# Turning x and h of a graph network by DMA crossbar transfers instead of TensorE

## The chip, the cores and the metric

The kernel runs on one core of a Trainium2 chip. The metric is the device time in microseconds (us); before the change it is 2685.53 us, the median of three runs (2683.47 to 2687.09). The engines are PE (TensorE, matmul), DVE (VectorE), ACT (ScalarE), POOL (GpSimd) and SP (SyncE, which here only issues DMA transfers).

## The reference

The input x is 128 graphs of 128 nodes with 256 features, in fp32; adj is a 128x128 adjacency matrix per graph. Four layers follow each other, each with a residual sum and a layer norm over the features. Layer 0 is a gated graph network of three steps, layers 1 to 3 are attention layers on the graph.

```python
# layer 0
A = (adj != 0)
h = x
for i in range(3):
    m = h @ weight[i]
    aggr = einsum('bst,bsd->btd', A, m)
    gi = aggr @ w_ih.T + b_ih
    gh = h @ w_hh.T + b_hh
    r = sigmoid(i_r + h_r); z = sigmoid(i_z + h_z)
    n = tanh(i_n + r * h_n)
    h = (1 - z) * n + z * h
x = layernorm(x + h)
# layers 1 to 3, in outline
Wh = x @ W.T
e = leaky_relu(Wh @ a1 + (Wh @ a2).T), masked where adj == 0
x = layernorm(x + softmax(e) @ Wh)
```

## The kernel before

The 128 graphs are worked on in 32 groups of 4 (G = 4), so that a tile of 128 partitions has 4 x 128 = 512 columns (GN). The 256 features are two halves of 128 (KC = 2, index c).

A group goes through gru() (layer 0) and then gat() (layers 1 to 3). gru() needs the node state h in two layouts. In rows (nodes on partitions, features along the row) h is the stationary operand of the aggregation at line 526, A transposed times h. Turned (features on partitions, the nodes of 4 graphs along the row) it is the moving operand of the gate products at line 473, and the elementwise work on the gates is done in this layout too. So x, which is loaded in rows, is turned at the start (transposed(), line 372; the PE transposes at line 380), and the new h, which arises turned, is brought back to rows after steps 0 and 1 (line 607). After step 2 the same line 607 turns h for the layer norm. A PE transpose is a matmul against the identity of one 128x128 block; four of them fill a PSUM bank, and one copy of 128x512 (line 287 on ACT or 289 on DVE, by copy()) takes the bank to an SBUF tile.

The gate products use a scheme with 7 block products in place of 8 (strassen(), line 456; sums(), line 433, makes the sums of the moving operand on GpSimd or DVE, line 443). A gate bank is emptied by lines 534, 538 and 541 on ACT and line 478 on DVE. The new h is made by lines 568 to 591; line 586 may run on GpSimd or DVE. In gat(), lines 711 and 722 are the two matmuls of the attention, 648 and 681 its PE transposes.

The order of the work is planned before the build. Every operation is given to the class Plan with the engines that may do it and an assumed duration for each, the tiles it reads and writes, and a priority (by group). Plan.order() starts operations one after another on the engine that is free, with assumed hand-over times (LATENCY: 250 for PE, 220 ACT, 200 DVE, 250 POOL, 4000 SP, in ns, and a margin of 300 ahead of PE), and the instructions are emitted in this order. Each engine then works through its own list strictly in order; an instruction whose inputs are not there holds everything behind it on its engine. Buffers come from pools of fixed size: "gate" and "bank" are the 8 PSUM banks, "k2" are SBUF tiles of 128x512 fp32, "k4" of 128x1024. `own` sets how many buffers of a pool the older of the groups in work keeps for itself.

In the steady part of the run gru() of one group and gat() of another share PE. The last four groups (LAST = 4) are ordered step by step instead of group by group.

Of the kernel before, what the change touches and what calls it, by code (L numbers as in the profile page):

```python
# [14 lines left out]
P = 128  # L15
D = 256
KC = D // P
G = 4
GN = G * P
H = GN // 2  # L20
STEPS = 3
# [177 lines left out]
def adj_resnorm_kernel(  # L199
# [14 lines left out]
    nc = tc.nc  # L214
    B = x.shape[0]
    NG = B // G
    LAST = 4
# [3 lines left out]
    psum = ctx.enter_context(tc.tile_pool(name="psum", bufs=1, space=bass.MemoryType.PSUM))  # L221


    pools = {"gru": 5, "xs": 2, "adj": 2, "am": 5, "k2": 26, "k4": 18, "fx": 2, "jx": 2, "f": 4, "mv": 4, "st": 6, "v": 24,
             "gate": 5, "bank": 3}
    own = ({"k2": 12, "k4": 5, "gate": 2, "v": 5, "fx": 0, "jx": 0, "st": 0}, {"k2": 4, "k4": 3, "v": 5, "fx": 0, "jx": 0, "st": 0})
    floats = {"gru": 0, "k4": 1024, "xs": 1024, "fx": 256, "jx": 256, "f": 8, "mv": 8, "st": 6, "v": 4}
    tags = {t: (n, floats.get(t, 512)) for t, n in pools.items()}
    BOTH = ("DVE", "POOL")
    plan = Plan({t: n for t, (n, _) in tags.items()}, own)  # L230
    slots = {t: [(psum if t in ("gate", "bank") else work).tile([P, w], I32 if t == "adj" else F32, name=f"{t}{i}")
# [2 lines left out]
    def T(b):  # L234
        if b.at is None:
            width = 1
            for s in b.shape:
                width *= s
            at = slots[b.tag][b.slot][:, 0:width]
            if len(b.shape) == 2:  # L240
                at = at.rearrange("p (a b) -> p a b", b=b.shape[-1])
            elif len(b.shape) == 3:
                at = at.rearrange("p (a b c) -> p a b c", b=b.shape[-2], c=b.shape[-1])
            b.at = at
        return b.at

    def bank():
        return Buf("bank", GN)
# [36 lines left out]
    def copy(e, dst, src):  # L285
        if e == "ACT":
            nc.scalar.copy(dst, src)  # L287
        else:
            nc.vector.tensor_copy(dst, src)  # L289

    LAND = 1500
    EVICT = {"ACT": 490, "DVE": 600}
    EVICT2 = {"ACT": 370, "DVE": 350}

    def load(dst, src, prio, start=0):
# [50 lines left out]
    def score_weights(l, prio):  # L346

        gatw, b_ = Buf("k2", KC, D), bank()
        load(gatw, gat_w[:, l], prio, start=30000)
        plan.op({"SP": 450}, lambda e: nc.sync.dma_start(T(gwT)[:, l], gat_wT[:, l]), writes=[(gwT, l)], prio=prio,  # L350
                lag=LAND, start=30000)

        for k in range(KC):
            st, mv = Buf("st", 6), Buf("mv", G, 2)
            plan.op({"DVE": 330}, lambda e, k=k, st=st: nc.vector.bn_stats(T(st), T(gwT)[:, l, k, :]),
                    reads=[(gwT, l)], writes=[st], prio=prio)
            plan.op({"DVE": 110}, lambda e, st=st, mv=mv: nc.vector.bn_aggr(T(mv)[:, 0, :], T(st)),
                    reads=[st], writes=[mv], prio=prio)
            plan.op({"DVE": 330}, lambda e, k=k, mv=mv: nc.vector.tensor_scalar(
                T(gwT)[:, l, k, :], T(gwT)[:, l, k, :], T(mv)[:, 0, 0:1], None, op0=ALU.subtract),  # L360
                reads=[mv, (gwT, l)], writes=[(gwT, l)], prio=prio)

        def fn(e):
            for h in range(2):
                for k in range(KC):
                    nc.tensor.matmul(T(b_)[:, h * D:(h + 1) * D], ga[:, l, k, h:h + 1].to_broadcast([P, P]),
                                     T(gatw)[:, k, :], start=(k == 0), stop=(k == KC - 1))
        plan.op({"PE": 4 * 432}, fn, reads=[gatw], writes=[b_], prio=prio)
        plan.op(EVICT, lambda e: copy(e, T(wa)[:, l, :, :].rearrange("p h d -> p (h d)"), T(b_)),
                reads=[b_], writes=[(wa, l)], prio=prio)  # L370

    def transposed(src, src_of, prio):

        res = []
        for c in range(KC):
            b_, dst = bank(), Buf("k2", GN)

            def fn(e, b_=b_, c=c):
                for b in range(G):
                    nc.tensor.transpose(T(b_)[:, b * P:(b + 1) * P], src_of(b, c), ident)  # L380
            plan.op({"PE": 440}, fn, reads=[src], writes=[b_], prio=prio)
            plan.op(EVICT, lambda e, b_=b_, dst=dst: copy(e, T(dst), T(b_)), reads=[b_], writes=[dst], prio=prio)
            res.append(dst)
        return res
# [48 lines left out]
    def sums(ms, prio):  # L433
# [5 lines left out]
        for j, (a, b, reads) in enumerate((  # L439
# [3 lines left out]
                nc.vector if e == "DVE" else nc.gpsimd).tensor_tensor(T(t)[:, j, :], a(), b(), ALU.subtract),  # L443
                reads=reads, writes=[(t, j)], prio=prio, port=BOTH)
        return t
# [53 lines left out]
    def gru(g, stage):  # L499

        xs, adj_i, am = Buf("xs", G, D), Buf("adj", G, P), Buf("am", G, P)
        prio = stage(g, 0)
# [4 lines left out]
                writes=[adj_i], prio=prio)  # L507
        if g == 0:
            input_weights(0, prio)
            hidden_weights(prio)  # L510
        plan.op({"DVE": 417}, lambda e: nc.vector.tensor_scalar(T(am), T(adj_i), 0, None, op0=ALU.not_equal),
                reads=[adj_i], writes=[am, turn], prio=prio, port=BOTH)
        hT = transposed(xs, lambda b, c: T(xs)[:, b, c * P:(c + 1) * P], prio)
        h = None
        for i in range(STEPS):
            prio = stage(g, i)
# [13 lines left out]
            last = i == STEPS - 1  # L530
# [15 lines left out]
            hT2 = []  # L546
            for c in range(KC):

                o, v, d = rz[c], nn[c], Buf("k2", GN)
# [4 lines left out]
                for gt in range(2):  # L554
                    if c == 0:
                        plan.op({"ACT": 630}, lambda e, gt=gt, o=o, tanh=tanh: tanh(gt, 0, GN, lambda: T(o)[:, gt, :]),
                                reads=[(o, 0), (o, 1)], writes=[(o, 2 + gt)], prio=prio)
                    else:
                        plan.op({"ACT": 365}, lambda e, gt=gt, tanh=tanh, rz=rz: tanh(
                            gt, 0, H, lambda: T(rz[2])[:, gt * H:(gt + 1) * H]),  # L560
                            reads=[rz[2]], writes=[(o, 4 + gt)], prio=prio)
                        plan.op({"ACT": 400}, lambda e, gt=gt, o=o, tanh=tanh: tanh(gt, H, GN, lambda: T(o)[:, gt, H:GN]),
                                reads=[(o, 1), (o, 4 + gt)], writes=[(o, 2 + gt)], prio=prio)
                if c == 1:
                    plan.op({"ACT": 370}, lambda e, v=v, nn=nn: nc.scalar.activation(
                        T(v)[:, 0, 0:H], T(nn[2])[:, 0:H], AF.Identity, bias=bhn[:, 1:2]),
                        reads=[nn[2]], writes=[(v, 0)], prio=prio)
                plan.op({"DVE": 620}, lambda e, o=o, v=v: nc.vector.scalar_tensor_tensor(  # L568
                    T(v)[:, 0, :], T(o)[:, 0, :], 1.0, T(v)[:, 0, :], op0=ALU.add, op1=ALU.mult),
                    reads=[(o, 2), (v, 0), (v, 1)], writes=[(v, 2)], prio=prio, port=BOTH)  # L570
                if c == 0:
                    plan.op({"DVE": 620}, lambda e, v=v: nc.vector.tensor_add(T(v)[:, 0, :], T(v)[:, 1, :], T(v)[:, 0, :]),
                            reads=[(v, 2)], writes=[(v, 3)], prio=prio, port=BOTH)
                else:
                    plan.op({"DVE": 350}, lambda e, v=v, nn=nn: nc.vector.tensor_add(
                        T(v)[:, 0, 0:H], T(nn[2])[:, H:GN], T(v)[:, 0, 0:H]),
                        reads=[(v, 2), nn[2]], writes=[(v, 3)], prio=prio)
                    plan.op({"DVE": 350}, lambda e, v=v: nc.vector.tensor_add(  # L578
                        T(v)[:, 0, H:GN], T(v)[:, 1, H:GN], T(v)[:, 0, H:GN]),
                        reads=[(v, 2)], writes=[(v, 4)], prio=prio, port=BOTH)  # L580
                plan.op({"ACT": 630}, lambda e, v=v, c=c: nc.scalar.activation(  # L581
                    T(v)[:, 0, :], T(v)[:, 0, :], AF.Tanh, bias=bin_[:, c:c + 1]),
                    reads=[(v, 3), (v, 4)], writes=[(v, 5)], prio=prio)

                plan.op({"POOL": 1250, "DVE": 610}, lambda e, d=d, v=v, h_=hT[c]: (
                    nc.vector if e == "DVE" else nc.gpsimd).tensor_tensor(T(d), T(h_), T(v)[:, 0, :], ALU.subtract),  # L586
                    reads=[hT[c], (v, 5)], writes=[d], prio=prio, port=BOTH)
                plan.op({"DVE": 620}, lambda e, d=d, o=o: nc.vector.scalar_tensor_tensor(  # L588
                    T(d), T(o)[:, 1, :], 1.0, T(d), op0=ALU.add, op1=ALU.mult),
                    reads=[(o, 3), d], writes=[d], prio=prio, port=BOTH)  # L590
                plan.op({"DVE": 620}, lambda e, d=d, v=v: nc.vector.scalar_tensor_tensor(
                    T(d), T(d), 0.5, T(v)[:, 0, :], op0=ALU.mult, op1=ALU.add),
                    reads=[d, (v, 5)], writes=[d], prio=prio, port=BOTH)
# [6 lines left out]
            else:  # L600
                h2 = [Buf("k2", G, P) for c in range(KC)]
            for c in range(KC):
                b_ = bank()

                def fn(e, b_=b_, c=c, hT2=hT2):
                    for b in range(G):
                        nc.tensor.transpose(T(b_)[:, b * P:(b + 1) * P], T(hT2[c])[:, b * P:(b + 1) * P], ident)  # L607
                plan.op({"PE": 440}, fn, reads=[hT2[c]], writes=[b_], prio=prio)
                if last:
                    plan.op({"DVE": 620}, lambda e, b_=b_, c=c, y=y: nc.vector.tensor_add(  # L610
                        T(y)[:, :, c * P:(c + 1) * P], T(b_).rearrange("p (b d) -> p b d", b=G),
                        T(y)[:, :, c * P:(c + 1) * P]), reads=[b_, turn, (y, 0)],
                        writes=[(y, b) for b in range(G)], prio=prio)
                else:
                    plan.op(EVICT, lambda e, b_=b_, c=c, h2=h2: copy(
                        e, T(h2[c]), T(b_).rearrange("p (b d) -> p b d", b=G)), reads=[b_], writes=[h2[c]], prio=prio)
            if not last:
                h, hT = h2, hT2
# [4 lines left out]
    def gat(g, xc, no, stage):  # L623
# [3 lines left out]
        for l in range(3):  # L627
# [64 lines left out]
            else:  # L692
                plan.op(EVICT, lambda e, b_=b_, pT=pT: copy(e, T(pT).rearrange("p b j -> p (b j)"), T(b_)),
                        reads=[b_], writes=[pT], prio=prio)
# [45 lines left out]
    def stage(g, n):  # L740

        tail = NG - LAST
        return g if g < tail else tail + n, 2 * g + (n >= STEPS)

    for g in range(NG):
        gat(g, *gru(g, stage), stage)
# [47 lines left out]
```

## Time and profile before

| what | value | how to read it |
|---|---|---|
| time | 2685.53 us | median of 3 runs |
| span of the profiled run | 2682.8 us | from first to last instruction |
| granted TensorE clock | 0.996 | share of full speed, so nothing is throttled |
| bank copies of 128x512 on ACT, line 287 | 396 of 587 ns | the copies after PE transposes are among them |
| the same on DVE, line 289 | 218 of 688 ns | |
| loads of x in rows | 32 of 512 KB, 3.8 us | from the issue to the landing |
| loads of adj | 32 of 256 KB, 2.8 us | the same |

Busy time of an engine is an average over the whole span; whether it matters is seen in the chain of work that ended last and in the idle time of PE. A matmul's row gives the time from its start to its end, and several are in flight at once: 128x256 products take 380 ns each by their row and follow each other every 216 ns. One matmul instruction in fp32 appears as two passes in the trace, a transpose as one.

### The profile page before, as it was taken

To read this page: it belongs to the slowest core of one execution; us is meant where nothing else is said; L and a number is where in the kernel's file an instruction comes from. 1 tells how busy PE (TensorE), PEld (TensorE's weight loads), DVE (VectorE), ACT (ScalarE), POOL (GpSimd) and SP (SyncE) were. 2 spreads that over 40 slices of the span, in tenths; PEclk is the share of its full clock that TensorE was granted. 3 is DMA by queue.
4 is the path that set the end of the run, shared out by engine and by line. 5 is a ranking of instruction groups with operands and counts; after the bars stand their busy time and mean duration, and the time that the engine had idled before them with its cause. 6 is when DMAs were issued, how large, how long until landed. Compare 5 with 4: busy or idle time off the path is not lost.

```text
span 2682.8 us, 41895 instructions
## 1 busy us (share of the span) xinstructions
PE 2650.4 (99%) x14536; PEld 2367.5 (88%) x14536; DVE 2069.0 (77%) x6111; ACT 1611.6 (60%) x4453; POOL 549.7 (20%) x618
## 2 busy tenths in 40 slices
PE   8999999999999999999999999999999999999988
PEld 7888888898898888898889888988988898988877
DVE  5677677887777877778877778777878777786787
ACT  4555666565656666566556566656666665655467
POOL 1122122221122221122211122211222211231111
PEclk9999999999999999999999999999999999999999
DMA  3100000000000000000000001000000000000000
GB/s 110 32 17 20 28 13 28 21 25 28 14 27 21 24 28 21 21 28 21 24 28 21 21 20 28 24 22 19 29 21 25 28 21 17 19 6 24 17 1 32
DMA packets 70102, 65.35 MB, mean 24 GB/s; under 512 B 2689, under 2 KB 68225, under 8 KB 69889
## 3 DMA queue, kind: packets, MB, share of 16 engines
q1 hardware_dynamic: 69456, 62.66, 7.7%
q8 instruction: 114, 1.87, 0.3%
q14 instruction: 100, 0.81, 0.1%
q10 hardware_dynamic: 432, 0.01, 0.0%
HBM read 45.89 MB, written 16.78 MB: 23 GB/s over the span
## 4 chain that ended last, share of the span: by engine, by line
PE 93%; DVE 4%; ACT 1%; issue 1%; DMA 0%; POOL 0%; POOLq 0%; SPq 0%; ACTq 0%; DVEq 0%
PE gate L473 63%; PE bank L722 11%; PE bank L526 6%; PE bank L711 6%; PE bank L607 3%; PE bank L681 1%; PE bank L648 1%; DVE fx L635 1%; PE bank L380 1%; PE bank L338 1%; DVE k L728 1%; DVE k L289 0%; DVE k L568 0%; DVE k L478 0%; DVE k L653 0%
## 5 line engine op out<-in xcount | busy, mean ns | idle before, releaser
L473 PE MATMUL gate<-k,whs 128*128 128x256 f32 x4032 | 1201.1, 380 | 2.4 <-DVE k L478 1.9
L473 PE MATMUL gate<-k,wcs 128*128 128x256 f32 x4032 | 1199.2, 379 | 0.0
L473 PEld LDWEIGHTS gate<-k,wcs 128*128 128x128 f32 x4032 | 766.1, 190 | 104.0
L473 PEld LDWEIGHTS gate<-k,whs 128*128 128x128 f32 x4032 | 730.4, 190 | 84.5 <-DVE k L478 3.1
L478 DVE TENSOR_TENSOR k<-gate,k 128x512 f32<-128x512 f32 x576 | 389.3, 684 | 207.9 <-PE gate L473 184.0
L287 ACT COPY k<-bank 128x512 f32<-128x512 f32 (+1 forms) x401 | 229.5, 584 | 206.8 <-PE bank L607 91.3
L722 PE MATMUL bank<-gwT,k 128*128 128x256 f32 x1536 | 348.8, 380 | 1.0 <-DVE k L289 0.8
L722 PEld LDWEIGHTS bank<-gwT,k 128*128 128x128 f32 x1536 | 290.4, 190 | 42.2 <-DVE k L289 1.8
L552 ACT ACTIVATE k<-k,brz 128x512 f32<-128x512 f32 (+1 forms) x384 | 225.6, 622 | 166.3 <-DVE k L478 164.7
L389 POOL TENSOR_TENSOR v<-v,neghalf 128x4 f32<-128x4 f32 x128 | 134.4, 1050 | 857.7 <-DVE v L428 840.3
L635 DVE SCALAR_TENSOR_TENSOR fx<-k,wa 128x256 f32<-128x256 f32 x768 | 285.9, 426 | 24.3 <-ACT k L408 24.2
L417 ACT ACTIVATE jx<-k 128x256 f32<-128x256 f32 x384 | 156.5, 408 | 231.0 <-DVE k L728 230.7
L534 ACT COPY k<-gate 128x512 f32<-128x512 f32 x288 | 167.6, 582 | 192.8 <-PE gate L473 188.4
L443 POOL TENSOR_TENSOR k<-k,k 128x256 f32<-128x256 f32 x229 | 175.9, 789 | 450.0 <-DVE k L289 223.2
L728 DVE SCALAR_TENSOR_TENSOR k<-bank,v,k 128x256 f32<-128x256 f32 x384 | 167.2, 476 | 106.8 <-PE bank L722 106.6
L289 DVE COPY k<-bank 128x512 f32<-128x512 f32 x219 | 150.1, 686 | 114.0 <-PE bank L711 88.6
L586 POOL TENSOR_TENSOR k<-k,k 128x512 f32<-128x512 f32 x90 | 133.3, 1492 | 303.4 <-ACT k L581 284.2
L711 PEld LDWEIGHTS bank<-k,k 128*128 128x128 f32 x1536 | 187.6, 194 | 7.7 <-DVE k L728 1.9
L711 PE MATMUL bank<-k,k 128*128 128x128 f32 x1536 | 191.2, 278 | 2.2 <-DVE k L728 1.1
L588 DVE SCALAR_TENSOR_TENSOR k<-k,k 128x512 f32<-128x512 f32 x192 | 170.1, 886 | 2.2 <-POOL k L586 1.1
L674 ACT ACTIVATE k<-k,v 128x128 f32<-128x128 f32 x384 | 148.9, 389 | 30.8 <-DVE v L670 30.2
L581 ACT ACTIVATE k<-k,bi 128x512 f32<-128x512 f32 x192 | 138.3, 721 | 47.1 <-DVE k L578 36.9
(86 smaller groups left out, 3012.9 us busy)
## 6 DMA issues: line engine op xcount, KB each, us to landing
xs<-in_x_dram SPq DMA_DIRECT2D x32, 512.0 KB, 3.8
k<-in_x_dram SPq DMA_DIRECT2D x32, 512.0 KB, 3.8
out_dram<-k SPq DMA_DIRECT2D x32, 512.0 KB, 2.9
adj<-in_adj_dram SPq DMA_DIRECT2D x32, 256.0 KB, 2.8
k<-in_gnn_wT_dram SPq DMA_DIRECT2D x3, 256.0 KB, 4.8
k<-in_w_ihT_dram SPq DMA_DIRECT2D x2, 384.0 KB, 5.8
k<-in_w_hhT_dram SPq DMA_DIRECT2D x2, 384.0 KB, 6.0
k<-in_gat_w_dram SPq DMA_DIRECT2D x3, 256.0 KB, 4.6
```

The source lines that it names most:

```text
L287: nc.scalar.copy(dst, src)
L443: nc.vector if e == "DVE" else nc.gpsimd).tensor_tensor(T(t)[:, j, :], a(), b(), ALU.subtract),
L473: nc.tensor.matmul(T(dst)[:, j * H:(j + 1) * H], T(w)[:, m, gt, :], moving(m, ms)[1](), start=first and n == 0, stop=n == len(todo) - 1, s ...
L478: plan.op({"DVE": 630}, lambda e: nc.vector.tensor_add(T(o)[:, :, j * H:(j + 1) * H], T(b_).rearrange("p (g n) -> p g n", g=2), T(part).re ...
L526: nc.tensor.matmul(T(b_)[:, b * P:(b + 1) * P], src, T(am)[:, b, :], start=True, stop=True)
L534: plan.op({"ACT": 500}, lambda e: nc.scalar.copy(T(dst), T(src)), reads=[src], writes=[(dst, 0), (dst, 1)], prio=prio)
L552: nc.scalar.activation(T(o)[:, gt, n0:n1], src(), AF.Tanh, bias=brz[:, gt * KC + c:gt * KC + c + 1], scale=0.5)
L588: plan.op({"DVE": 620}, lambda e, d=d, o=o: nc.vector.scalar_tensor_tensor(T(d), T(o)[:, 1, :], 1.0, T(d), op0=ALU.add, op1=ALU.mult), rea ...
L635: plan.op({"DVE": 345}, lambda e, b=b, h=h, l=l, f=f, fx=fx, xc=xc: nc.vector.scalar_tensor_tensor(T(fx), T(xc)[:, b, :], 1.0, T(wa)[:, l, ...
L711: nc.tensor.matmul(T(b_)[:, b * P:(b + 1) * P], T(xc)[:, b, c * P:(c + 1) * P], T(pT)[:, b, :], start=True, stop=True)
L722: nc.tensor.matmul(T(b_)[:, (b - b0) * D:(b - b0 + 1) * D], T(aT[k])[:, b * P:(b + 1) * P], T(gwT)[:, l, k, :], start=(k == 0), stop=(k == ...
L728: nc.vector.scalar_tensor_tensor(T(y)[:, b, :], T(b_)[:, (b - b0) * D:(b - b0 + 1) * D], T(rden)[:, b:b + 1], T(xc)[:, b, :], op0=ALU.mult ...
```

## The change

The turn of x (for groups 2 to 31) and the return of h to rows (after steps 0 and 1 of groups 0 to 27) are taken off PE. The crossbar of the DMA engines can transpose[...]. So turned() does it in three operations: a copy takes the fp32 words apart into a tile of all low 16-bit halves followed by all high halves; one transfer issued by SP transposes the 8 blocks of 128x128 halves into a second tile (rows); a copy puts low and high halves together again into the first tile. The copies run on ACT or DVE. Nothing is rounded: the halves are moved as integers. x of groups 0 and 1, h of the last four groups and the turn after step 2 stay on PE.

With this the pools are divided anew: 4 gate and 4 other PSUM banks in place of 5 and 3, one k2 tile more and one adjacency tile fewer, and other reserves for the older group. The planner gives the transfer 1200 ns on SP and then SP's hand-over time of 4000 ns, and the copies 1000 ns on ACT and 620 on DVE. The whole order comes out anew from it. The purpose is to relieve PE of these transposes.

```diff
-    pools = {"gru": 5, "xs": 2, "adj": 2, "am": 5, "k2": 26, "k4": 18, "fx": 2, "jx": 2, "f": 4, "mv": 4, "st": 6, "v": 24,
-             "gate": 5, "bank": 3}
-    own = ({"k2": 12, "k4": 5, "gate": 2, "v": 5, "fx": 0, "jx": 0, "st": 0}, {"k2": 4, "k4": 3, "v": 5, "fx": 0, "jx": 0, "st": 0})
+    pools = {"gru": 5, "xs": 2, "adj": 2, "am": 4, "k2": 27, "k4": 18, "fx": 2, "jx": 2, "f": 4, "mv": 4, "st": 6, "v": 24,
+             "gate": 4, "bank": 4}
+    own = ({"k2": 6, "k4": 5, "gate": 1, "bank": 1, "v": 5, "fx": 0, "jx": 0, "st": 0}, {"k2": 3, "k4": 1, "bank": 1, "v": 5, "fx": 0, "jx": 0, "st": 0})
...
+    U16 = mybir.dt.uint16
...
+    APART = {"ACT": 1000, "DVE": 620}
+    TURN = 0
...
+    def turned(src, key, dst, shape, prio):
+        rows = Buf("k2", GN)
+        flat = lambda: T(dst) if shape else T(dst).rearrange("p b q -> p (b q)")
+        halves_of = lambda at: at.bitcast(U16).rearrange("p (h b q) -> p h b q", h=2, b=G)
+        pairs_of = lambda at: at.bitcast(U16).rearrange("p b (q h) -> p h b q", h=2)
+        plan.op(APART, lambda e: copy(e, halves_of(flat()), pairs_of(src())), reads=[key], writes=[dst], prio=prio, port=BOTH)
+        plan.op({"SP": 1200}, lambda e: nc.sync.dma_start_transpose(
+            T(rows).bitcast(U16).rearrange("p (a q) -> p a q", q=P), flat().bitcast(U16)),
+            reads=[dst], writes=[rows], prio=prio, lag=TURN)
+        plan.op(APART, lambda e: copy(e, pairs_of(T(dst).rearrange(shape, b=G) if shape else T(dst)), halves_of(T(rows))),
+                reads=[rows], writes=[dst], prio=prio, port=BOTH)
...
-        hT = transposed(xs, lambda b, c: T(xs)[:, b, c * P:(c + 1) * P], prio)
+        if g < 2:
+            hT = transposed(xs, lambda b, c: T(xs)[:, b, c * P:(c + 1) * P], prio)
+        else:
+            hT = [Buf("k2", GN) for c in range(KC)]
+            for c in range(KC):
+                turned(lambda c=c: T(xs)[:, :, c * P:(c + 1) * P], xs, hT[c], "p (b q) -> p b q", prio)
...
             for c in range(KC):
+                if not last and g < NG - LAST:
+                    turned(lambda c=c, hT2=hT2: T(hT2[c]).rearrange("p (b q) -> p b q", b=G), hT2[c], h2[c], None, prio)
+                    continue
                 b_ = bank()
...
-        return g if g < tail else tail + n, 2 * g + (n >= STEPS)
+        return (g + (0 if n >= STEPS else 0) if g < tail else tail + n), 2 * g + (n >= STEPS)
```

## The prediction

> **What bounds the kernel now.** I read the engine shares and the slices first, then the windows of one steady group, then the chain, then the groups of the lines that the change touches, then the timeline around one transpose.
>
> ```profile
> PE 2650.4 (99%) x14536; PEld 2367.5 (88%) x14536; DVE 2069.0 (77%) x6111; ACT 1611.6 (60%) x4453; POOL 549.7 (20%) x618
> ...
> PE   8999999999999999999999999999999999999988
> ```
>
> PE is busy for 99% of the span; only the first slice and the last two fall short. A busy PE row alone proves little, since pipelined matmuls overlap, so the next view is one steady group in numbers (columns: span of the stretch, then busy time and instruction count of PE, PEld, DVE, ACT, POOL, then granted clock, DMA share, GB/s):
>
> ```profile
> 0.00:60.00 60.00, 51.95 (x230) 41.51 (x231) 34.55 (x74) 26.92 (x54) 11.99 (x19) 0.97 0.38 123
> 1081.60:1163.20 81.60, 81.60 (x453) 73.36 (x452) 64.17 (x192) 49.79 (x140) 16.86 (x19) 1.00 0.08 24
> 2550.00:2683.00 133.00, 114.33 (x626) 97.47 (x624) 108.01 (x500) 93.27 (x331) 21.16 (x25) 0.94 0.05 17
> ```
>
> The steady group (the chain's runs of gate products repeat every 81.6 us) leaves PE no idle time, DVE 17 us, ACT 32 us; the DMA engines are 92% free. PE idles only in the first 60 us (8) and the last 133 us (19).
>
> ```profile
> PE 93%; DVE 4%; ACT 1%; issue 1%; DMA 0%; POOL 0%; POOLq 0%; SPq 0%; ACTq 0%; DVEq 0%
> ...
> L607 PE MATMUL bank<-ident,k 128*128 128x128 f32 x768 | 115.9, 274 | 2.3 <-ACT k L287 1.5 <-DVE k L591 0.7 <-DVE k L728 0.2
> L380 PE MATMUL bank<-ident,xs 128*128 128x128 f32 x256 | 39.1, 280 | 8.3 <-DMA xs<-in_x_dram 8.0 <-ACT k L287 0.2
> ```
>
> 93% of the chain is PE: removing PE work shortens the kernel one for one until another wait appears. Lines 607 and 380 are the transposes. Their 274 ns is the time of one, not what it takes from the queue; that is read from start to start:
>
> ```profile
> 1199.92 0.60 PE L607 MATMUL bank<-ident,k 128*128 128x128 f32 x4
> ...
> 1200.36 0.60 PE L473 MATMUL gate<-k,whs 128*128 128x256 f32 x2
> ...
> 1200.56 0.59 ACT L287 COPY k<-bank 128x512 f32<-128x512 f32 x1 [1.54 <-PE bank L607]
> ```
>
> Four transposes start at 1199.92 and the next product at 1200.36: 0.44 us for one half (c) of a group. The copy out of the bank takes 0.59 us.
>
> **What the Trainium skill says.** (1) "TensorE: Matmul & The Clock Gate", Part 4: a PE transpose of 128x128 takes about 275 ns in a kernel. The trace agrees as to duration (274), but pipelined it costs 110 ns of the queue, and that is what a saving is counted in. (2) "VectorE: DVE Perf Modes", Mode 2×_2P: a one-source copy between SBUF tiles runs at two elements a cycle. The trace agrees for one such shape: line 511 takes 420 ns for 512 elements where the two-source line 591 takes 689. No 16-bit copy with a step of two is in the trace. (3) Same page, The three transpose paths: 1309 ns for a crossbar transpose of one 128x128 of 2-byte elements. (4) "DMA: Bandwidth & Descriptors", Latency and other measured facts: 261 GB/s for crossbar transposes. No run of before shows either; where the two are far apart my range is wide.
>
> **The change, part by part.**
>
> *PE work removed.* x of groups 2 to 31 (30 groups x 2 halves = 60) and h after steps 0 and 1 of groups 0 to 27 (28 x 2 x 2 = 112): 172 sets. The built instruction lists agree: 172 crossbar transposes, 688 fewer matmuls. 172 x 0.44 = 75.7 us, 2.64 us of each 81.6 us group. All of it is on the chain.
>
> *Copies.* 172 bank copies leave, by the lists 94 from ACT and 78 from DVE; 344 copies of 1024 16-bit elements come, 238 on ACT and 106 on DVE. ACT: line 287 at 384 elements from SBUF takes 512 ns and grows by 0.84 ns an element (372 at 256, 587 at 512), so 512 + 640 x 0.84 = 1.05 us. DVE: line 511 gives 0.16 us fixed plus 0.51 ns an element, so 0.68 us; if the halved rate isn't granted for a step of two, 1.2 us. I take 0.68, because both sides are in SBUF and there is one source. Per steady group that is 8 more on ACT and 4 on DVE: ACT 49.8 + 8 x 1.05 - 3.3 x 0.59 = 56 of 79 us, DVE 64.2 + 4 x 0.68 - 2.7 x 0.69 = 65 of 79. Neither becomes the bound; as busy time the copies hide beside PE.
>
> *The transfer.* Its 256 KB at 6 a group put 1.5 MB on engines that are 92% free. Its latency is what counts. Lower bound: the plain 256 KB load of adj lands in 2.8 us and a 512 KB load in 3.8, so the slope is 1.0 us for 256 KB (262 GB/s, the rate the skill gives for transposes). Upper bound: the fixed 1.8 us plus eight blocks one after another at the skill's price, 1.8 + 8 x 1.31 = 12.3. I take 4 us, near the lower end: the rate quoted for a whole transfer says more of 256 KB than the price of one lone block, in which fixed cost is large; the 1.2 over the plain load is for the many small pieces of a 16-bit transpose.
>
> *The wait it adds.* Before, a finished half of h reached the next aggregation after one PE slot and one copy (0.44 + 0.6, and some latency). Now it passes copy, transfer, copy. I read the window in the built order of a steady group, with the changed kernel's line numbers: 490 is the gate product, 548 the aggregation, 608 and 613 the first and last operation on the new h, 736 and 747 the two attention products. I count PE slots (0.43 us a matmul of 256 columns, 0.21 of 128, from start to start) from the last PE work which the first copy must wait for to the matmul of line 548 that reads the result, and place the ACT and DVE instructions in front of each copy at their durations. Step 0 to 1, c = 0: PE gives 9.5 us (10 matmuls of line 490, 8 of 736, 8 of 747); line 613 and the first copy use 2.7, the second copy and its handoff 1.3, so the transfer must land within 5.5 us. c = 1: PE gives 12.4, the chain through GpSimd's line 608 uses 4.6, again the second copy 1.3: 6.5. Step 1 to 2: over 8 (c = 0) and about 6.4 (c = 1). x is turned long before its first use: more than 70 us of PE slots. So at 4 us no PE instruction waits; it takes more than 5.5. The second copy stands in its engine's queue, mostly ACT's: if the transfer is late, gate copies (lines 556 and 560) behind it wait too, and PE behind these; but they have 1 to 4 us of slack of their own.
>
> *Other edits.* One bank moves from gates (5 to 4) to banks (3 to 4), one adjacency buffer goes for one more k2: cost nothing themselves; in the built order a gate bank is still emptied about 1.5 us before PE reuses it, which work of the other group hides. The line in stage() adds zero.
>
> *Sum.* 2685.5 - 75.7 = 2609.8. The windows are short in places, so I add 0.1 us for each of 112 turned halves of h for jitter: 11 us. Forecast 2621.
>
> **Rivals.**
>
> *Landing at 7.5 us or more.* The first copy of the next step is then 2 us late at one boundary in each of 2 steps of 28 groups, and since c = 1 is later anyway, a stall that delays all of PE also widens its window: 56 x 2 = 112 us lost against 75.7 gained: 2609.8 + 11 + 112 = 2733, slower; at 12.3 us it is 56 x 6.8 = 381, about 3000. For it: the price of a lone block, and that the transfer works in 16-row tiles (64 of them by the built list). Against: the rate for whole transfers, and idle DMA engines.
>
> *Landing at 6 to 6.5 us, or DVE copies at full length (1.2 us).* Some 0.7 us a boundary: 2621 + 56 x 0.7 = 2660. Still faster. For it: the windows are nowhere more than 1 us wider than 5.5 on the short side; GpSimd and DVE already disturb each other (line 588 takes 886 ns where the same shape at line 591 takes 689).
>
> *Gate banks become the wait.* With 4, a late gate copy stops PE: 0.1 us on each of 42 products of a group is 4.2 us against 2.64 won, 28 x 1.6 = 45 us slower: 2730. Against: ACT and DVE both have spare time, and the margin in the order is 1.5 us.
>
> **How the numbers follow.** Forecast 0.58; landing at 6 to 6.5 or slow copies 0.15; late landing 0.21; gate banks 0.06. Faster: 0.58 and 0.14 of the second case, 0.72; within 0.2% 0.03, its last 0.01 and 0.02 of the late landings, since a latency near 6.7 us cancels the gain; slower 0.19 + 0.06 = 0.25. Low end 2600: all 75.7 us and 10 of the 27 us that PE idles at the ends. High end 2735: this takes in the second case, the gate banks and landings up to 7.5 us, and leaves out the longer ones, some 0.12, and a little below.
>
> **What would show it.** Right: in a steady group the period falls to about 79 us with PE still without idle; the page's DMA issues show the crossbar transfers landing in 3.5 to 5.5 us; lines 397 and 632 hold 16 and 320 transposes instead of 256 and 768; ACT's copies of 1024 elements take about 1.05 us and DVE's about 0.68. Wrong: PE of line 548 or the second copies of line 288 wait on DMA for tens of us in sum, or line 490 waits on the ACT and DVE copies of gates. A landing over 5.5 us, or DVE over 90% busy, would make the prediction wrong.

## The result and the profile after

| | before | after |
|---|---|---|
| time, median of the runs beside each other | 2685.19 us (2683.47 to 2687.09) | 2620.9 us (2620.57 to 2621.04) |
| span of the profiled run | 2682.8 us | 2618.9 us |
| granted TensorE clock | 0.996 | 0.995 |

The ratio is 0.976, with a 95% interval of 0.9743 to 0.9777: 64.3 us faster. The forecast was 2621.

The page of the changed kernel, first the engine shares and PE's slices:

```profile
PE 2578.3 (98%) x13848; PEld 2297.8 (88%) x13848; DVE 2084.6 (80%) x6162; ACT 1817.4 (69%) x4572; POOL 535.0 (20%) x602
...
PE   8999999999999999999999999999999999999988
```

688 matmuls have gone and PE's busy time fell by 72.1 us; ACT took on 205.8 us of work and DVE 15.6, and the span still fell by 63.9. The windows of the changed kernel (columns as in the prediction: busy time and count of PE, PEld, DVE, ACT, POOL, then clock, DMA share, GB/s):

```profile
200.00:500.00 300.00, 294.84 (x1588) 261.31 (x1587) 243.92 (x699) 213.21 (x529) 70.58 (x85) 1.00 0.18 44
1079.00:1158.00 79.00, 79.00 (x431) 70.85 (x429) 64.58 (x192) 57.09 (x144) 17.06 (x19) 1.00 0.19 44
2240.00:2290.00 50.00, 45.50 (x242) 39.91 (x241) 41.10 (x119) 31.03 (x85) 10.74 (x11) 0.96 0.04 12
2490.00:2619.00 129.00, 107.45 (x611) 93.60 (x609) 107.38 (x491) 87.52 (x312) 20.56 (x24) 0.94 0.05 17
```

The steady group has no PE idle time in its 79 us either. ACT's 57.09 and DVE's 64.58 stand where 56 and 65 were forecast. The chain repeats at the new period:

```profile
1009.33 8.64 PE gate L490 x40
...
1088.31 8.64 PE gate L490 x40
```

From start to start that is 78.98 us against 81.6 before. Next the DMA issues of the changed kernel (count, median us from issue to landing), and the trace's account of the line that issues the transfers (least, median and greatest):

```profile
adj<-in_adj_dram SPq DMA_DIRECT2D x32, 256.0 KB, 2.8
...
k<-k SPq DMA_TRANSPOSE x172, 3.1
```

```profile
L383 SPq DMA_TRANSPOSE k<-k x172: 1231/1238/2427, 19.6 to 2232.1; - x172
...
DMA to landing us min/median/max: 3.0/3.1/4.9
```

A transfer lands 3.1 us after its issue, 0.3 us more than the plain load of 256 KB from DRAM, and holds SP for 1.24 us. The copies, by line, engine and tile (least, median and greatest ns):

```profile
L288 ACT COPY k<-k x203: 1029/1336/1419, 24.6 to 2235.4; 128x1024 uint16<-128x1024 uint16 x102
...
L288 ACT COPY k<-xs x35: 1029/1044/1052, 18.1 to 2230.6; 128x1024 uint16<-128x1024 uint16 x35
```

```profile
L290 DVE COPY k<-k x81: 677/694/1253, 24.6 to 2235.6; 128x1024 uint16<-128x1024 uint16 x81
...
L290 DVE COPY k<-xs x25: 659/680/693, 61.8 to 2230.0; 128x1024 uint16<-128x1024 uint16 x25
```

The group from xs holds only first copies, which read with a step of two; the group from k holds both kinds. By the built list 39 of ACT's 203 and 73 of DVE's 81 are first copies, so ACT's median is near that of its 164 second copies, which write with a step of two (1.34 us, 1.33 in the window below), and DVE's is that of its first copies, 0.69. DVE's 8 second copies take 0.73 to 0.77. A single first copy on DVE took 1.25 us; why is not shown. Two of DVE's, one second and one first:

```profile
258.31 0.74 DVE L290 COPY k<-k 128x1024 uint16<-128x1024 uint16 x1
...
259.72 1.25 DVE L290 COPY k<-k 128x1024 uint16<-128x1024 uint16 x1
```

One short window of the changed kernel, c = 0 at the boundary from step 1 to step 2 (start, duration, engine and line). The prediction and the expectations have the names of the two boundaries exchanged: they call this one "step 0 to 1". In the built list this half, once aggregated, goes on to wcs[2], the weights of the third step. The sums in the prediction are those of the right transfers; from here on the names are by the built list.

```profile
1184.26 1.05 ACT L288 COPY k<-k 128x1024 uint16<-128x1024 uint16 x1
...
1185.34 5.46 SPq L383 DMA_TRANSPOSE k<-k  x2
...
1190.55 1.33 ACT L288 COPY k<-k 128x1024 uint16<-128x1024 uint16 x1
```

The second line merges two transfers; the first is issued at 1185.34 and has landed 3.1 us later, at 1188.4. ACT comes to the second copy only at 1190.55, since two activations of line 574 stand before it, and ends at 1191.9; PE reads the result at line 548 from 1193.14, after the hand-over and a weight load (0.45 us together). The copy could have started some 0.8 us later still, so the transfer had about 6.0 us. The forecast gave it 5.5.

The narrowest window is another one, c = 1 from step 0 to step 1:

```profile
1223.96 0.69 DVE L290 COPY k<-k 128x1024 uint16<-128x1024 uint16 x1
...
1229.31 1.41 ACT L288 COPY k<-k 128x1024 uint16<-128x1024 uint16 x1
...
1231.39 1.05 PE L548 MATMUL bank<-am,k 128*128 128x128 f32 x8
```

The first copy ends at 1224.65, ACT comes to the second 4.7 us later, and PE follows 0.67 us after that copy, hardly more than the 0.45 it needs. All four halves in the steady part, in us after the end of the first copy:

| half | ACT comes to the second copy | latest landing that delays no PE product | forecast |
|---|---|---|---|
| step 0 to 1, c = 0 | 4.1 | 12.2 | over 8 |
| step 0 to 1, c = 1 | 4.7 | 4.9 | 6.4 |
| step 1 to 2, c = 0 | 5.2 | 6.0 | 5.5 |
| step 1 to 2, c = 1 | 5.9 | 6.6 | 6.5 |

At 3.1 us the transfer is ahead of all of these.

*An account used below.* A busy PE row hides small gaps, because matmuls overlap. So I count slots, from start to start in the traces: 0.216 us for each 256-column pass, 0.111 for each 128-column pass, 0.11 for a transpose. What the span has beyond the slots are gaps. They hold PE's waits and also the passes that took twice their slot, which are found where the granted clock stands at 0.5 (8.0 of the 62.1 us after; more on this under the repeated transfers).

| kernel | span | PE slots | gaps |
|---|---|---|---|
| before | 2682.8 | 2632.5 | 50.3 |
| after | 2618.9 | 2556.8 | 62.1 |

The slots fell by 75.7, the gaps rose by 11.8, and the difference is the 63.9 us of the spans.

### The profile page after: what moved, and what is told of

Same layout as the page of the kernel before. It is cut to its first block, busy times and chain, and to the rows that moved or that the text cites. A ratio compares the mean times of both kernels' runs of the same rounds, so it can differ in the third digit from the quotient of the medians.

```text
span 2618.9 us, 41369 instructions
## 1 busy us (share of the span) xinstructions
PE 2578.3 (98%) x13848; PEld 2297.8 (88%) x13848; DVE 2084.6 (80%) x6162; ACT 1817.4 (69%) x4572; POOL 535.0 (20%) x602
## 3 DMA queue, kind: packets, MB, share of 16 engines
q1 hardware_dynamic: 251088, 107.77, 17.2%
## 4 chain that ended last, share of the span: by engine, by line
PE 92%; DVE 6%; ACT 1%; issue 1%; DMA 0%; POOLq 0%; SPq 0%; ACTq 0%; DVEq 0%
PE gate L490 64%; PE bank L747 11%; PE bank L736 6%; PE bank L548 6%; DVE fx L660 1%; PE bank L706 1%; PE bank L673 1%; PE bank L632 1%; DVE k L753 1%; PE bank L341 1%; DVE k L290 1%; DVE k L495 0%; DVE k L610 0%; DVE k L678 0%; DVE k L590 0%
## 5 line engine op out<-in xcount | busy, mean ns | idle before, releaser
L460 POOL TENSOR_TENSOR k<-k,k 128x256 f32<-128x256 f32 x251 | 214.5, 862 | 557.0 <-DVE k L460 236.3
L574 ACT ACTIVATE k<-k,brz 128x256 f32<-128x256 f32 (+1 forms) x384 | 225.1, 621 | 134.8 <-DVE k L495 134.8
L288 ACT COPY k<-k 128x1024 uint16<-128x1024 uint16 x203 | 257.7, 1290 | 10.8 <-DVE k L613 7.8
L288 ACT COPY k<-bank 128x512 f32<-128x512 f32 (+1 forms) x307 | 177.2, 581 | 115.7 <-PE bank L736 48.0
L610 DVE SCALAR_TENSOR_TENSOR k<-k,k 128x512 f32<-128x512 f32 x192 | 143.4, 748 | 40.9 <-POOL k L608 39.9
L560 ACT ACTIVATE k<-gate,bhn 128x256 f32<-128x256 f32 x288 | 135.9, 472 | 50.7 <-PE gate L490 47.2
```

The lines of the kernel that those rows point to most:

```text
L574: nc.scalar.activation(T(o)[:, gt, n0:n1], src(), AF.Tanh, bias=brz[:, gt * KC + c:gt * KC + c + 1], scale=0.5)
```

## The experiments

The theory: PE slots are what the change saves; the landing of 3.1 us stays below the windows, so nothing waits. The rivals: the saving comes from another part (pools, new order), or the transfers do cost and something else pays for it. Where a kernel has a line number a little off, its edit moved the lines.

### One part at a time, with the order planned anew

*pools_only*: the changed kernel's pools, with all transposes on PE.

```diff
-        if g < 2:
+        if True:
...
-                if not last and g < NG - LAST:
+                if False:
```

> All transposes stay on PE; only the new division of the pools and reserves is taken over (gate 4, bank 4, k2 27, am 4). Theory: PE is the bound and the pools move nothing by themselves, so 2685 us, within 5. Rival: the new division itself costs what is missing between 75.7 us of PE slots removed and 64 us gained (about 2697), or brings part of the gain itself (under 2675).

Measured 2735.83, ratio to before 1.0192 (1.0176 to 1.0207): 50 us slower with the same PE work. "Cost nothing themselves" is refuted for the pools as such.

*x_only*: only x goes by the crossbar (the second edit alone). *h_only*: only h does (the first edit alone).

> The changed kernel with only x turned by the crossbar (60 sets), h goes back to PE. Theory: 60 sets at 0.44 us, 2685.5 - 26.4 = 2659 us, within 5, since x has time. Rival: the gain comes from the freed banks and the new order and isn't in proportion to the sets: over 2670 or under 2645.

> The changed kernel with only h turned by the crossbar (112 sets), x goes back to PE. Theory: 112 sets at 0.44 us, 2685.5 - 49.3 = 2636 us; up to 11 us more if the short windows cost anything. Rival: turning h in the chain of steps loses most of it to waits: over 2660.

Measured 2713.68 (1.0107, 1.0092 to 1.0122) and 2713.34 (1.0101, 1.0085 to 1.0118). Both are slower than before, although each takes work from PE.

*last_too*: the turn after step 2 goes by the crossbar too, and DVE adds the result to y.

```diff
-                if not last and g < NG - LAST:
+                if g < NG - LAST:
+                    if last:
+                        h2 = [Buf("k2", G, P) for c in range(KC)] if c == 0 else h2
                     turned(...)
+                    if last:
+                        plan.op({"DVE": 620}, lambda e, ...: nc.vector.tensor_add(
+                            T(y)[:, :, c * P:(c + 1) * P], T(h2[c]), T(y)[:, :, c * P:(c + 1) * P]), ...)
```

> The changed kernel, with the turn of h after step 2 taken off PE as well for groups 0 to 27 (56 sets more), followed by the sum with x out of SBUF. Theory (PE is still the bound and DVE and ACT have room): 2621 - 56 x 0.44 = 2596 us. Rival: the latency now stands ahead of the attention layers, and four more copies a group crowd ACT and DVE (both then near 60 and 68 of 78 us): 2610 to 2640.

Measured 2742.34 (1.0217, 1.0202 to 1.0232), and not below the changed kernel.

*plan_true*: the same work as the changed kernel; the planner is told that a transfer takes 3.2 us in all in place of 5.2, which is nearer to the 3.1 measured.

```diff
-    TURN = 0
+    TURN = -2000
```

> The changed kernel planned anew with a transfer of 3.2 us, about what it takes, instead of 5.2. Theory: PE never waited in the steady part, so nothing is to be had there: 2621 us, at most 5 less at the ends. Rival: the reserve of 2 us held buffers and cost part of the missing 11 us: about 2611.

Measured 2721.25 (1.0134, 1.0119 to 1.0149): 100 us slower than the changed kernel with the same operations, only in another order and with 120 copies on DVE in place of 106. Its PE waits (us in all, times, longest):

```profile
PE gate L490 <- DVE k L495: 18.4, 26, 1.7
PE bank L548 <- ACT k L288: 18.2, 9, 4.5
```

In the changed kernel these two are 1.8 and 1.0 us. All five kernels have large gaps, a term that I hadn't priced; with the slots known, it stands for how well the planned order packs:

| kernel | span | PE slots | gaps |
|---|---|---|---|
| pools_only | 2732.2 | 2632.5 | 99.7 |
| x_only | 2712.7 | 2606.1 | 106.6 |
| h_only | 2711.3 | 2583.2 | 128.1 |
| last_too | 2740.4 | 2532.2 | 208.2 |
| plan_true | 2715.5 | 2556.8 | 158.7 |

The passes at half the clock are 31 us of the gaps of last_too and 10 to 20 in the other four. These kernels can't price the parts: each changes a part and the fit of the order with it. What was needed was kernels with a held order, and kernels with an order fitted to their own work.

### At a held order

*pe_work_back*: the changed kernel in its own order, with the 688 transposes put back on PE as added work. They stand ahead of the aggregation and write the bank that it overwrites, so nobody waits for them.

```diff
+                    if more:
+                        for b in range(G):
+                            nc.tensor.transpose(T(b_)[:, b * P:(b + 1) * P],
+                                                T(xs)[:, b, c * P:(c + 1) * P] if h is None else T(h[c])[:, b, :], ident)
                     for b in range(G):
```

> The changed kernel in its own order, with 688 PE transposes put in again without a use (ahead of the aggregation, into the bank that the aggregation then overwrites), so that crossbar, copies and pools are as changed but PE has its old work. Theory: 2621 + 688 x 0.11 = 2697 us, within 8; so the gain is PE's slots and nothing else. Rival (the gain comes from the new order and pools): under 2670.

Measured 2693.56, ratio to before 1.0032 (1.002 to 1.0044). Against the changed kernel that is 72.7 us for 688 transposes, 106 ns each, where the slots said 110. The steady group of this kernel:

```profile
1000.00:1081.60 81.60, 81.60 (x454) 73.25 (x453) 64.69 (x192) 57.39 (x144) 16.80 (x19) 1.00 0.18 43
```

Again 81.60 us without PE idle. In the changed kernel's order PE work counts one for one. The change is therefore two terms: -72.7 us of PE work and, from 2684.2 (before, beside this run) to 2693.6, +9.4 us for all the rest: new order, pools, copies and transfers.

*one_of_four*: the kernel before in its own order; for the 172 sets only one transpose of four is done. The other three blocks of each are left out and hold stale values.

```diff
-                for b in range(G):
+                for b in range(sets):
                     nc.tensor.transpose(T(b_)[:, b * P:(b + 1) * P], src_of(b, c), ident)
```

> The kernel before in its own order, with three of the four PE transposes of each of the 172 sets left out (so three quarters of these blocks are not turned; everything else, bank copies too, stays). It prices PE's slots by themselves. Theory (93% of the chain is PE, so slots count one for one at 0.11 us a transpose): 2685 - 516 x 0.11 = 2628 us, within 5. Rival (other engines set the pace of the order as soon as PE is relieved, as the replanned variants might suggest): over 2655.

Measured 2658.12 (0.9899, 0.9883 to 0.9916): 26 us gained where 516 x 0.11 = 56.8 us of slots went. So in the old order the saving is not one for one. The weight loads of PE, which run just ahead of the matmuls, show who holds them, first in this kernel, then in the kernel before:

```profile
PEld bank L681 <- ACT k L674: 19.6, 33, 4.0
PEld bank L607 <- DVE k L591: 19.2, 71, 0.7
```

```profile
PEld bank L681 <- ACT k L674: 7.0, 8, 4.0
...
PEld bank L607 <- DVE k L591: 2.2, 6, 0.7
```

The chain has 9% of DVE now, against 4% before. The waits are short, 0.27 us a time at line 607, and there were 71 of them: in the old order DVE's work on the new h was only some tenths of a us behind PE. The bank copies, which the change takes away too, stay in this kernel; how much of the 31 us not gained is theirs isn't tested.

### With an order fitted to the work

*h_fit* and *last_fit*: h_only and last_too, with pools and reserves chosen for them by the planner's own assumed end.

```diff
-    pools = {..., "am": 4, "k2": 27, "k4": 18, ..., "gate": 4, "bank": 4}
+    pools = {..., "am": 5, "k2": 24, "k4": 19, ..., "gate": 5, "bank": 3}
```

```diff
-    pools = {..., "am": 4, "k2": 27, "k4": 18, ..., "gate": 4, "bank": 4}
+    pools = {..., "am": 4, "k2": 27, "k4": 18, ..., "gate": 5, "bank": 3}
```

(The reserves in `own` were chosen anew in both.)

> Only h by the crossbar, as in the run of that kind which came out 28 us slower than the kernel before, but with a division of pools and reserves fitted to this set of operations (5 gate and 3 other banks, k2 24, k4 19, am 5). Theory (that run lost to an order that doesn't fit, not to turning h): 2636 us by its 112 sets, at most 15 more. Rival (turning h in the chain of steps itself costs more than it saves when x isn't turned): 2690 or more.

> The turn after step 2 by the crossbar too (228 sets in all), with pools and reserves fitted to it (5 gate banks, 3 others). Theory: 2621 - 56 x 0.44 = 2596 us, at most 15 more, faster than the changed kernel. Rival (the latency ahead of the attention layers and the copies cost it whatever the order): 2621 or more.

| kernel | time | ratio to before | slots | gaps | gaps of the unfitted one |
|---|---|---|---|---|---|
| h_fit | 2676.07 | 0.9967 (0.9954 to 0.998) | 2583.2 | 91.0 | 128.1 |
| last_fit | 2634.31 | 0.9811 (0.9797 to 0.9826) | 2532.2 | 100.1 | 208.2 |

Fitting is worth 37 and 108 us: the slowness of h_only and last_too was mostly their order and pools. But neither comes to the 50 to 62 us of gaps that before and after have. h_fit falls between the two values expected and settles nothing about the share of h; last_fit is on the rival's side, still 13 us behind the changed kernel with 24.6 us fewer slots. PE's waits of last_fit:

```profile
PE bank L547 <- ACT k L287: 20.4, 52, 0.8
PE gate L489 <- DVE k L494: 7.8, 29, 0.6
```

52 waits of 0.4 us for the second copy on ACT. It takes 1.34 us where the planner assumes 1.00, and the planner's margin ahead of PE is 0.30. That this is the cause is argued, not shown: a plan with 1.34 wasn't run.

### How close the transfers are

*twice_h* and *thrice_h*: each transfer of h is issued two or three times in a row, the order of the work being the same. *thrice_x*: the same for x, three times. The repeated transfers write the same values again, and each waits for the one before it.

```diff
+        def turn(e):
+            for _ in range(1 if shape else 2):
+                nc.sync.dma_start_transpose(
+                    T(rows).bitcast(U16).rearrange("p (a q) -> p a q", q=P), flat().bitcast(U16))
+        plan.op({"SP": 1200}, turn, reads=[dst], writes=[rows], prio=prio, lag=TURN)
```

> The changed kernel in the same order, but each transfer of h is issued twice into the same tile, the second after the first has landed, so that the result is there after about 6.2 instead of 3.1 us. Theory (a window of 5.5 us at the step from 0 to 1, wider ones after it): 0.7 us lost at 28 to 56 boundaries, 2641 to 2660 us; if the window is 6 us, as the profile of the changed kernel suggests, 2627 to 2632. Rival (the transfer is hidden whatever it takes, the windows are far wider): 2621.

> As with two transfers of h, but three, so about 9.3 us, and the second half of h waits on SP for the first half's repeats. Theory: some 6 us lost at the step from 0 to 1 and 3 at the next, 28 x 9 = 250 us, 2870 us; with only the late landing and no queueing 56 x 3.8 = 213, 2834. Rival (hidden): under 2650.

> The changed kernel in the same order, each transfer of x issued three times one after another, those of h once. Theory as predicted (x is needed only 70 us of PE slots later): 2621 us. Rival (what counts is the place of the second copy in ACT's queue: it holds the gate copies behind it until the transfer lands, here 9 us after its issue for the first half and 17 for the second, where the order leaves 5): 5 to 12 us lost for each of 28 groups, 2760 to 2950.

| kernel | landing of the last, from the half's first issue | time | ratio to before | over the changed kernel |
|---|---|---|---|---|
| twice_h | 2 x 3.1 = 6.2 us | 2713.11 | 1.0106 (1.009 to 1.0121) | 92 us, 3.3 a group |
| thrice_h | 3 x 3.1 = 9.3 us | 3100.01 | 1.1544 (1.1527 to 1.1562) | 479 us, 17 a group |
| thrice_x | 9.3 us | 2952.47 | 1.1001 (1.0983 to 1.102) | 331 us, 12 a group |

All three are worse than the forecast's own formula. At 6.2 us it gave 0.7 us for each of 56 boundaries, 39 us; there were 92. At 9.3 it gave 56 x 3.8 = 213; there were 479. And x, which was to have 70 us, should have cost nothing; the rival put down before the run, that the place of the second copy in ACT's queue counts, gave 2760 to 2950. Repeats also stand in front of other transfers on SP: in thrice_x the second half of x lands 16 us after its first copy. The waits of twice_h (line 550 is the aggregation):

```profile
ACT k L288 <- DMA k<-k: 137.8, 82, 3.8
...
PE bank L550 <- ACT k L288: 58.9, 39, 3.7
```

In the changed kernel the first of these is 2.0 us in 3 times. The second is PE waiting at the first use of the result, and 38.7 of its 58.9 us are for the narrowest half, step 0 to 1, c = 1: a landing of 6.3 us after the first copy is too late for its 4.9. ACT for its part is held at all four halves. What an ACT that waits does is seen in twice_h's timeline (in brackets: idle before it, and who ended it):

```profile
1273.00 1.35 ACT L288 COPY k<-k 128x1024 uint16<-128x1024 uint16 x1 [2.00 <-DMA k<-k]
...
1274.21 0.41 ACT L436 ACTIVATE jx<-k 128x256 f32<-128x256 f32 x1
```

This copy belongs to step 0 to 1, c = 0, the half with the widest window by PE (12.2 us). PE didn't need it yet; but ACT stands still for 2 us, and the squares (line 436) behind it are late. In the changed kernel the same copy stands between two pairs of squares without idle time. The chain of thrice_x shows it whole, one piece after another in order of time:

```profile
1207.86 3.04 DMA k<-k
...
1210.92 3.21 DMA k<-k
...
1214.24 1.33 ACT k L288
1215.56 0.45 ACT k L558
...
1216.06 7.48 PE gate L492 x20
```

Two transfers in turn, the copy on ACT, behind it a gate copy (line 558), and only that releases PE: the gate bank is free. PE did not wait for x here. In this kernel ACT waits 330.6 us for DMA in 57 times, and all but 2.0 us of it is for the repeated transfers of x, not for those of h that stand behind them on SP. PE waits at the gate products 206.2 us for ACT's gate copies in 26 times, and at the aggregation only 8.9 us. So the time that a transfer has ends at the place of the waiting copy in ACT's queue or at the first use of its result, whichever stops PE first: for x in thrice_x it was the queue, in twice_h both took part.

In these runs a stop of PE cost more than its length. The end of the same wait in thrice_x, on PE (each line is two passes):

```profile
1216.06 1.22 PE L492 MATMUL gate<-k,whs 128*128 128x256 f32 x2 [8.66 <-ACT k L558]
1217.07 1.06 PE L492 MATMUL gate<-k,wcs 128*128 128x256 f32 x2
1217.92 1.06 PE L492 MATMUL gate<-k,whs 128*128 128x256 f32 x2
...
1222.08 0.59 PE L492 MATMUL gate<-k,wcs 128*128 128x256 f32 x2
1222.51 0.59 PE L492 MATMUL gate<-k,whs 128*128 128x256 f32 x2
```

The trace has a granted clock of 0.5 from 1211.5 to 1221.7, and in it the passes follow each other every 0.43 us in place of 0.216. Such passes took 68 us beyond their slots in thrice_x and 117 in thrice_h, against 8 in the changed kernel and 18 in twice_h; the mean granted clock fell to 0.948 and 0.946. So this is some 60 of the 331 us, 109 of the 479 and 10 of the 92; the larger part is the waiting itself.

## Why the prediction was right, point by point

- *The bound.* PE work taken away shortens the changed kernel one for one: confirmed at its order (106 ns for a transpose by pe_work_back, 110 forecast). As a rule for the kernel before, "one for one until another wait appears", it holds much less far than I read it: in the old order one_of_four brought 46% (26 of 56.8 us). That PE had no idle time in the steady group said nothing of how near the next wait was. The new order, not the removal alone, made the saving whole.
- *PE work removed.* 172 x 0.44 = 75.7 us: shown as 72.7 by pe_work_back. The period of 79 us came as forecast, lines 397 and 632 hold 16 and 320 transposes.
- *Copies.* DVE right, 0.68 to 0.69 for first copies and 0.73 to 0.77 for the 8 second ones: the two elements a cycle that the Trainium skill ("VectorE: DVE Perf Modes", Mode 2×_2P) gives for one-source copies fit these times for 16-bit elements with a step of two, where the slow rate of the prediction would have been 1.2. ACT's first copies are right (1.04 to 1.05), the second ones mis-sized: 1.34. 164 of them, 0.29 us longer than forecast, are 48 us of ACT in all; they lie beside PE.
- *Landing.* 3.1 us for 4 forecast, within the bounds of 2.8 and 12.3, and below the 3.5 to 5.5 that I said the profile would show. The price of a lone block in the Trainium skill (same page, The three transpose paths) can't be multiplied: eight of them would have made 10.5 us. The spare size of this term covered what others lacked: at the 4 us forecast, ACT would have come to one of the second copies with 0.1 us to spare.
- *The windows.* 6.0 for 5.5 at c = 0 of step 1 to 2 (under the exchanged name): right. But it isn't the narrowest: c = 1 of step 0 to 1 has 4.9 where 6.4 was forecast, so "it takes more than 5.5" is wrong by 0.6 us. The steps beside it fell: "turned long before its first use: more than 70 us of PE slots" and "they have 1 to 4 us of slack of their own". The prediction named the path, a copy in ACT's queue that blocks the gate copies behind it, but took it to have room; thrice_x cost 331 us where these two steps give nothing.
- *Other edits.* "Cost nothing themselves" fell for the pools taken alone, +50 us in pools_only. In the changed kernel, where pools and order belong together, everything besides the PE work came to +9.4 us.
- *The 11 us for jitter.* The gaps rose by 11.8 us, so the size was right; the place was wrong. The steady group has no PE idle. PE's idle time rose from 32.4 to 40.6 us: in the ramp (2.3 to 5.2 us between 200 and 500), around 2240 to 2290 where the last four groups begin (4.5), and in the end stretch (18.7 to 21.6). A right sum with a term in the wrong place is partly luck.
- *The rivals.* Late landing was real but doesn't happen at 3.1 us; its price was set at less than half of what twice_h and thrice_h cost, because one window was taken too wide, and neither the copies waiting in ACT's queue nor the clock after a stop of PE were priced. Gate banks as the wait: line 490 waits 1.8 us for line 495 in the changed kernel, so not there, but it is the first wait of plan_true.

*What stays open.* Why this order packs to 62 us of gaps, where plan_true has 159 with the same work and the fitted ones 91 and 100, isn't explained; nor can x and h be priced apart, as each needs its own order. No version here beat the changed kernel.

## What to carry to other kernels

Count a saving on a full engine in start-to-start slots, and then ask how near the next wait is: in the order laid out for the old load it was tenths of a us away here, and a new order collected the rest. Judge such an order by span less slots; orders of the same instructions differed by 100 us here. A transfer's window can end where the instruction that waits for it stands in its engine's queue, however late its result is needed: read both that place and the first use, for every transfer. And look at the granted clock after a stop of PE before pricing a stop by its length.

## What the runs showed of the hardware

- A crossbar transfer of 256 KB from SBUF to SBUF, eight 128x128 blocks of 16-bit halves, lands in 3.1 us (3.0 to 4.9), only 0.3 more than a plain load of 256 KB from DRAM, and holds its issuing queue for 1.24 us.
- It takes more of the DMA engines than plain transfers of its size: the queue's share rose from 7.7% to 17.2% of 16 engines' span, (0.172 x 2618.9 - 0.077 x 2682.8) / 172 = 1.42 us of all 16 engines for each. The plain transfers of the kernel before took 0.077 x 2682.8 = 207 us for 62.7 MB, 0.86 us for 256 KB.
- ACT copies 1024 16-bit elements in 1.04 us when it reads with a step of two, and in 1.34 us when it writes with one. On DVE the difference is small: 0.69 and 0.74.
- After a wait of PE of 8.66 us (thrice_x) the granted clock was 0.5 until 6 us after PE's restart, and a 256-column pass took 0.43 us in place of 0.216.
